# Gate and up of a block-quantized feed-forward as three products of 12-bit parts

## The chip, the cores and the metric

The program runs on one core of a Trainium2 chip. The core has five engines that run at the same time, each through its own queue in order: TensorE (PE) for matrix products, VectorE (DVE), ScalarE (ACT) and GpSimd (POOL) for elementwise work, and SyncE (SP), which here issues the DMA transfers. They wait for each other through semaphores. The metric is the time of one execution in microseconds (us) on the device. The kernel before takes 665.8 us, the median of three runs (665.08 to 667.82).

## The reference

`x` is 4 x 2048 tokens of 256 features. What is computed, cut to what matters:

```
xn   = layernorm(x)
s    = linear attention of xn over the tokens of a batch     (L2-normed Q, K; V; gamma)
gate = q(xn) @ q(w_gate).T          # 256 -> 704
up   = q(xn) @ q(w_up).T            # 256 -> 704
h    = silu(gate) * up
g    = silu(q(h) @ q(w_down).T)     # 704 -> 256
out  = x + (xn + gamma * weighted) * g
```

`q` is a blockwise 4-bit quantization and back: each block of 16 values is divided by its largest magnitude / 6, rounded to the grid 0, 0.5, 1, 1.5, 2, 3, 4, 6 and multiplied by the scale again. The result of `q` is a float32 number: a grid value times a float32 scale. `h` is quantized from the results of gate and up, so a gate or up that is off by a rounding can move a value of `h` to another grid point.

## The kernel before

The 8192 tokens are cut into 32 groups of 256 tokens (two tiles `t` of 128; NG = 8 groups a batch). A main loop `for s in range(3, N - 1)` runs a software pipeline by hand: the schedule is exactly the order of the program, and each engine works its own instructions in that order. In iteration `s` the parts of different groups are worked on:

- gate and up of group s+1 in six pieces (`pieces`, `gate_up`, L436): 2 token tiles x 3 chunks of columns (512, 512 and 384, gate and up interleaved by 64). A piece is 2 float32 products over the 256 features (the profile shows each float32 product as two instructions) into one of two PSUM banks of `ps_gu`. ACT then takes silu of the gate half (`si`, L451) and copies the up half (`up`, L453), POOL multiplies them into `h` (L455).
- the scaling of h of group s-1 (`scale_h`, L371): on DVE the largest magnitudes per block (`largest`, L151) of h and of the tokens of group s+3, the reciprocal, and h times it (`over`, L177, tile `y_h`); the same for the tokens (`y_x`).
- the rounding to the grid: ACT makes a 16-bit short of y (`short`, L210, tiles `t_h` and `t_x`), DVE four 16-bit operations (`on_grid`, L222 to L226), once for h and once for the tokens.
- the turn from tokens on the partitions to features on the partitions: the 16-bit grid values go through a DMA transpose each (`turn_q`, L415, tiles `qt_h`, `qt_x`); the scales are transposed on PE (`turn_scales`), written to DRAM (`there`) and read back spread over 16 rows of each block (`se`, L402).
- DVE multiplies the turned grid values by the spread scales: `rescale_x` (L419, tile `xqt`, group s+2) and `rescale_h` (L429, tile `hqt`, group s-2).
- down of group s-3 (`down`, L465): 12 float32 products of 256 columns (24 instructions), then silu on ACT (`gate_of`, L481).
- attention: `gram_step` (L327) for group s+3, `turn_xn` (L344) transposes its tokens; every eighth iteration the generator `attention` starts, which makes the batch's matrix M, advanced one step at each `turn()`; `preset` (L504) and `attend` (L511) for group s-7, then the product with the gate on DVE (`gated`, L521), the sum with x on POOL (`finish`, L528) and the store. `statistics`, `deviations` and `normalize` make the layer norm of later groups (mostly DVE, POOL and ACT).

Groups 0 to 4 are prepared ahead of the loop beside the weights: their tokens are quantized directly and turned on PE (`turn_xq`). The weights of gate and up are quantized in three chunks (`scale_gu`, `rounded`) and turned on PE into the tile `wgu` (`turn_gu`). After the loop a written-out end finishes the last groups.

All DMA transfers but one are issued by SP in program order: loads of x, the second load of x for the last sum (`xl`), the scales to DRAM and back, the transposes, the stores.

Of the kernel before, what the change touches and what calls it, by code (L numbers as in the profile page):

```python
# [10 lines left out]
F16 = mybir.dt.float16  # L11
AF = mybir.ActivationFunctionType
ALU = mybir.AluOpType
# [6 lines left out]
F16_EXPONENT = 0x7C00  # L20
DOWN = 1.0 - 3 * 2.0**-24
# [3 lines left out]
def kernel(  # L25
# [14 lines left out]
):  # L40

# [31 lines left out]
    ps_gu = ctx.enter_context(tc.tile_pool(name="ps_gu", bufs=2, space=bass.MemoryType.PSUM))  # L73
    ps_od = ctx.enter_context(tc.tile_pool(name="ps_od", bufs=2, space=bass.MemoryType.PSUM))
# [11 lines left out]
    def load_x(n: int):  # L86
        if n < N:
            xt = tok.tile([P, T, L], F32, tag="x", name=f"x_{n}", bufs=6)
            nc.sync.dma_start(xt, group_of(x, n))
            x_sb[n] = xt  # L90
# [3 lines left out]
    def reload_x(n: int):  # L94
        if 0 <= n < N:
            x_last[n] = tok.tile([P, T, L], F32, tag="xl", name=f"xl_{n}", bufs=3)
            nc.sync.dma_start(x_last[n], group_of(x, n))
# [5 lines left out]
    for j0, nb in chunks:  # L103
        w = tok.tile([P, HF], F32, tag="h", name=f"wgu_n{j0}", bufs=4)
# [25 lines left out]
    wd_n = tok.tile([P, NS * P], F32, tag="se", name="wd_n", bufs=2)[:, 0:HF]  # L130
# [12 lines left out]
    for i in range(5):  # L143
        xn = const.tile([P, T, L + 1], F32, tag=f"xn{i}", name=f"xn{i}")
        nc.gpsimd.memset(xn[:, :, L : L + 1], 1.0)
        xns.append(xn)
# [20 lines left out]
    def over(src: bass.AP, inv: bass.AP, F: int, kind: str, nm: str, sc=None):  # L167
# [5 lines left out]
        a = src.shape[1]  # L173
        most = T * L if kind == "x" else HF
        tag, bufs = {"x": ("yx", 2), "h": ("yh", 1), "w": ("hqt", 2)}[kind]
        y = tok.tile([P, most], F32, tag=tag, name=f"y_{nm}", bufs=bufs)[:, 0:F]
# [4 lines left out]
            inv.rearrange("p (a n) -> p a n", a=a).unsqueeze(3).to_broadcast([P, a, F // a // BLK, BLK]),  # L181
# [3 lines left out]
        return sc, y, F, kind, nm  # L185

    def scaled(src: bass.AP, F: int, kind: str, nm: str, multiplier=nc.vector):
        n, a = F // BLK, src.shape[1]
        most = T * L if kind == "x" else HF
        sc = small.tile([P, most // BLK], F32, tag="scx" if kind == "x" else "sch", name=f"sc_{nm}")[:, 0:n]  # L190
        largest(sc, src)
        inv = inverse(sc, nm)
        if multiplier is nc.vector:
            return over(src, inv, F, kind, nm, sc)
        nc.vector.tensor_scalar(inv, inv, DOWN, None, ALU.mult)
        y = tok.tile([P, most], F32, tag="hqt", name=f"y_{nm}", bufs=2)[:, 0:F]
        multiplier.tensor_tensor(
            y.rearrange("p (a n k) -> p a n k", a=a, k=BLK),
            src.rearrange("p a (n k) -> p a n k", k=BLK),
            inv.rearrange("p (a n) -> p a n", a=a).unsqueeze(3).to_broadcast([P, a, n // a, BLK]),  # L200
            ALU.mult,
        )
        return sc, y, F, kind, nm

    def short(state):
        sc, y, F, kind, nm = state
        most = T * L if kind == "x" else HF
        t = tok.tile([P, most], F16, tag="tx" if kind == "x" else "th", name=f"t_{nm}", bufs=2)[:, 0:F]
        upper = y.bitcast(BF16).rearrange("p (f two) -> p f two", two=2)[:, :, 1]
        nc.scalar.activation(t, upper, AF.Copy, scale=1.0 + 2.0**-9)  # L210
        return t

    def on_grid(state, t):
# [5 lines left out]
        sc, y, F, kind, nm = state  # L219
        most = T * L if kind == "x" else HF  # L220
        m = tok.tile([P, most], BF16, tag="mx" if kind == "x" else "mh", name=f"m_{nm}")[:, 0:F]
# [7 lines left out]
    def rounded(state, t, multiplier=nc.vector) -> bass.AP:  # L229

        return rescaled(state, on_grid(state, t), multiplier)

    def rescaled(state, q, multiplier=nc.vector) -> bass.AP:
        sc, y, F, kind, nm = state
        multiplier.tensor_tensor(
            y.rearrange("p (n k) -> p n k", k=BLK),
            q.rearrange("p (n k) -> p n k", k=BLK),
            sc.unsqueeze(2).to_broadcast([P, F // BLK, BLK]),
# [3 lines left out]

    def inv_sqrt(dst: bass.AP, v: bass.AP, nm: str):

        first = inv_sqrt_first(v, nm)
        inv_sqrt_steps(dst, v, *first)
# [89 lines left out]
    def turn_xn(n: int):  # L336
# [8 lines left out]
        xt = tok.tile([P, KC, GT], F32, tag="xnt", name=f"xnt_{n}", bufs=11)  # L345
# [6 lines left out]
    def scale_x(n: int):  # L352
        return scaled(tokens(n), T * L, "x", f"x{n}")

    def xqt_tile(n: int):
        tag, bufs = ("gate", 7) if n < 4 else ("xqt", 2)
        xqt[n] = tok.tile([P, T, KC, P], F32, tag=tag, name=f"xqt_{n}", bufs=bufs)
        return xqt[n].rearrange("p t c k -> p (t c k)")

    def turn_xq(n: int, xq: bass.AP):  # L360
# [4 lines left out]
        evict(xqt_tile(n), tp)  # L365
# [3 lines left out]
    scales, spread_sc, turned = {}, {}, {}  # L369

    def scale_h(n: int, m: int = N):  # L371
# [12 lines left out]
        inv_x[n] = inv[:, NIC * CB :]  # L384
        return over(src, inv[:, 0 : NIC * CB], HF, "h", f"h{n}")

    inv_x = {}

    def scale_x_of(n: int, h: int):
        return over(tokens(n), inv_x.pop(h), T * L, "x", f"x{n}")  # L390

    def turn_scales(key):
# [8 lines left out]
        se = tok.tile([P, NS * P], F32, tag="se", name=f"se_{key}", bufs=2)[:, 0 : n * BLK]  # L401
# [7 lines left out]
        se = se.rearrange("p (g t) -> p g t", t=P)  # L409
# [650 lines left out]
```

## Time and profile before

| | |
|---|---|
| median of the runs | 665.8 us |
| the profiled execution | 666.58 us |
| its span, first to last instruction | 664.8 us |
| granted TensorE clock | 0.997 |
| busy: PE, DVE, POOL, ACT | 639.3, 528.7, 320.5, 286.6 us |
| gate/up products (L442), 768 instructions | 315.9 us |
| down products (L469), 768 instructions | 171.0 us |
| start of loop iterations 3, 7, 29 (by the chain) | 85.35, 162.75, 586.58 us |

All times are of one profiled execution. A group in the profile reads: line, engine, operation, what it writes <- what it reads, shapes, count | busy time in total, mean ns of one | idle time of the engine just before it and what ended most of it. Matrix products are pipelined, so their mean ns overlap; the distance between starts tells what one costs in a stream. The chain follows back from the last instruction to what released each step.

### The profile page before, as it was taken

What the parts mean: (1) busy time and instruction counts of PE and PEld (TensorE: products, weight loads), DVE (VectorE), ACT (ScalarE), POOL (GpSimd) and SP (SyncE); (2) the same over time, 40 slices, a digit from 0 to 9 for tenths busy, and PEclk for the clock granted to TensorE, in tenths of its full rate; (3) what the DMA queues carried; (4) which work ended last, traced back from release to release, by engine and by line L of the source; (5) the groups of instructions that cost most, each with busy time, mean ns of one, the idle gap of its engine ahead of it and who ended that gap; (6) DMA issues with size and microseconds to landing.
All of it is one profiled execution on the core that took longest, in us unless ns stands there. A gap on an engine that the chain in (4) does not pass through costs nothing.

```text
span 664.8 us, 8117 instructions
## 1 busy us (share of the span) xinstructions
PE 639.3 (96%) x2486; PEld 435.3 (65%) x2486; DVE 528.7 (80%) x911; ACT 286.6 (43%) x701; POOL 320.5 (48%) x545
## 2 busy tenths in 40 slices
PE   3799999999999999999999999999999999999997
PEld 2446556656766666767666666766676666666886
DVE  6998997879866887867969786885997777888752
ACT  2366654344444444344453444444344444433230
POOL 5567445271635526264463636256263736537122
PEclk9999999999999999999999999999999999999999
DMA  9200488857489777764877888749778757884882
GB/s 228 77 17 0 54 101 138 117 53 85 103 122 140 140 115 108 127 99 119 137 112 101 135 125 130 120 121 141 84 113 126 111 113 114 120 125 72 150 176 97
DMA packets 86232, 74.19 MB, mean 112 GB/s; under 512 B 64076, under 2 KB 70444, under 8 KB 86188
## 3 DMA queue, kind: packets, MB, share of 16 engines
q1 hardware_dynamic: 85916, 73.40, 68.3%
q8 instruction: 20, 0.33, 0.2%
q10 hardware_dynamic: 272, 0.26, 0.1%
q14 instruction: 24, 0.20, 0.1%
HBM read 48.30 MB, written 10.27 MB: 88 GB/s over the span
## 4 chain that ended last, share of the span: by engine, by line
PE 83%; DVE 6%; POOL 3%; DMA 3%; ACT 2%; issue 1%; SPq 0%; DVEq 0%; ACTq 0%; POOLq 0%
PE gu L442 40%; PE dn L469 23%; PE at L511 8%; PE gram L327 5%; PE px L575 2%; PE tp_xn L344 2%; PE pm L661 1%; DMA qt_x<-t_x 1%; DMA wv_sb<-in_L_attn_Wv_dram 1%; DMA wgu_n<-in_L_ffn_w_gate_dram 1%; PE pa L640 1%; DMA x<-in_L_attn_x_dram 1%; POOL isq_r_ln L262 1%; PE tp_sc L396 0%; POOL h L455 0%
## 5 line engine op out<-in xcount | busy, mean ns | idle before, releaser
L442 PE MATMUL gu<-wgu,xqt 128*128 128x512 f32 (+1 forms) x768 | 315.9, 560 | 2.2 <-ACT xqt L314 2.2
L455 POOL TENSOR_TENSOR h<-si,up 128x256 f32<-128x256 f32 (+1 forms) x192 | 163.2, 857 | 274.4 <-ACT up L453 274.1
L442 PEld LDWEIGHTS gu<-wgu,xqt 128*128 128x128 f32 x768 | 143.0, 191 | 135.4 <-issue 105.4
L469 PE MATMUL dn<-wdt,hqt 128*128 128x256 f32 x768 | 171.0, 379 | 0.0
L469 PEld LDWEIGHTS dn<-wdt,hqt 128*128 128x128 f32 x768 | 144.2, 190 | 18.9
L451 ACT ACTIVATE si<-gu 128x256 f32<-128x256 f32 (+1 forms) x192 | 70.2, 366 | 192.2 <-PE gu L442 187.4
L419 DVE TENSOR_TENSOR xqt<-qt_x,se 128x512 f32<-128x512 bf16 x27 | 26.0, 961 | 72.0 <-DMA qt_x<-t_x 67.3
L453 ACT COPY up<-gu 128x256 f32<-128x256 f32 (+1 forms) x192 | 67.7, 353 | 0.0
L327 PEld LDWEIGHTS gram<-xn 128*128 128x128 f32 x256 | 44.0, 194 | 27.6 <-ACT xn L305 11.4
L511 PE MATMUL at<-M,xnt 128*128 128x256 f32 x256 | 59.7, 379 | 0.0
L429 DVE TENSOR_TENSOR hqt<-qt_h,se 128x1408 f32<-128x1408 bf16 x32 | 53.8, 1680 | 7.0 <-DMA qt_h<-t_h 7.0
L327 PE MATMUL gram<-xn 128*128 128x257 f32 (+1 forms) x256 | 48.9, 335 | 9.2 <-ACT xn L305 9.2
L177 DVE SCALAR_TENSOR_TENSOR y_h<-h,inv_h 128x1408 f32<-128x1408 f32 x32 | 54.7, 1711 | 2.5 <-ACT t_h L210 1.4
L210 ACT ACTIVATE t_h<-y_h 128x1408 f16<-128x1408 bf16 x32 | 44.3, 1385 | 17.5 <-DVE y_h L177 17.5
L151 DVE TENSOR_REDUCE scs<-h 128x88 f32<-128x1408 f32 x32 | 51.6, 1612 | 0.0
L511 PEld LDWEIGHTS at<-M,xnt 128*128 128x128 f32 x256 | 46.7, 190 | 6.7
L314 ACT COPY sct<-tp_sc 120x128 f32<-120x128 f32 (+1 forms) x32 | 8.4, 265 | 92.7 <-PE tp_sc L396 92.7
L305 ACT ACTIVATE xn<-x,shift,rstd 128x256 f32<-128x256 f32 x64 | 35.0, 597 | 28.2 <-POOL shift L295 28.2
L528 POOL TENSOR_TENSOR gate<-gate,xl 128x512 f32<-128x512 f32 x26 | 35.6, 1370 | 22.4 <-DVE gate L521 22.4
L225 DVE TENSOR_TENSOR t_h<-m_h,t_h 128x1408 bf16<-128x1408 bf16 x32 | 31.1, 972 | 1.1
L226 DVE TENSOR_TENSOR t_h<-t_h,m_h 128x1408 bf16<-128x1408 bf16 x32 | 28.5, 892 | 1.1
L164 DVE RECIPROCAL inv_h<-scs 128x120 f32<-128x120 f32 (+1 forms) x32 | 27.9, 873 | 1.1
(145 smaller groups left out, 662.9 us busy)
## 6 DMA issues: line engine op xcount, KB each, us to landing
se<-there SPq DMA_DIRECT2D x27, 960.0 KB
x<-in_L_attn_x_dram SPq DMA_DIRECT2D x32, 256.0 KB
out_dram<-gate SPq DMA_DIRECT2D x31, 256.0 KB
xl<-in_L_attn_x_dram SPq DMA_DIRECT2D x26, 256.0 KB
se<-there SPq DMA_DIRECT2D x5, 704.0 KB
there<-sct SPq DMA_DIRECT2D x27, 60.0 KB
wd_n<-in_L_ffn_w_down_dram SPq DMA_DIRECT2D x1, 704.0 KB
wgu_n<-in_L_ffn_w_up_dram SPq DMA_DIRECT2D x2, 256.0 KB
```

The source lines that it names most:

```text
L151: nc.vector.tensor_reduce(sc, src.rearrange("p a (n k) -> p a n k", k=BLK), AX.X, ALU.max, apply_absolute_value=True)
L177: nc.vector.scalar_tensor_tensor(y.rearrange("p (a n k) -> p a n k", a=a, k=BLK), src.rearrange("p a (n k) -> p a n k", k=BLK), DOWN, inv. ...
L210: nc.scalar.activation(t, upper, AF.Copy, scale=1.0 + 2.0**-9)
L327: nc.tensor.matmul(grams[b][:, o : o + L + 1 - c * P], xn[:, t, c * P : (c + 1) * P], xn[:, t, c * P : L + 1], start=(g == 0 and t == 0 an ...
L429: nc.vector.tensor_tensor(ht, turned.pop(("h", n)).rearrange("p g t -> p (g t)"), spread_sc[n][:, 0:NIC, :].rearrange("p g t -> p (g t)"), ...
L442: nc.tensor.matmul(gu[:, : nb * P], xqt[n][:, t, c, :], wgu[:, c, j0 * P : (j0 + nb) * P], start=(c == 0), stop=(c == KC - 1),)
L451: nc.scalar.activation(si[:, :nb, :], pair[:, :, 0, :], AF.Silu)
L453: nc.scalar.copy(up[:, :nb, :], pair[:, :, 1, :])
L455: nc.gpsimd.tensor_tensor(hs[n][:, o : o + nb * 64], si[:, :nb, :].rearrange("p j f -> p (j f)"), up[:, :nb, :].rearrange("p j f -> p (j f)"),
L469: nc.tensor.matmul(od[:, t, :], hqt[n][:, t * half + i, :], wdt[:, t * (half + 1) + i, :], start=(i == 0), stop=(i == half),)
L511: nc.tensor.matmul(ready[n][:, t, :], xt[:, c, t * P : (t + 1) * P], M[:, c, :], start=False, stop=(c == KC - 1), skip_group_check=True,)
L528: adder.tensor_tensor(gate, gate, x_last.pop(n), ALU.add)
```

## The change

**Gate and up.** For most groups (`SPLIT = 5, 5, 6`: from group 5 on for the first two chunks of columns, from group 6 on for the third) each float32 product is replaced by three products of type float32r. The tokens' tile f is split into a = f times (1 - 2^-13) rounded to float32r (`part_a`, ACT), b = f - a (`part_b`, POOL) and m = a - 2^12 b (`part_m`, DVE). The weights are split once, chunk by chunk, into three tiles `wgu[0..2]` (`split_gu`, six passes of ACT and four of POOL per chunk). A piece is now begun (`gu_begin`: a and b against the first two weight parts, four instructions), rescaled in PSUM by ACT (times 1 + 2^-12), and ended later in the program (`gu_end`: two more products of m, then si, up and h as before). Earlier groups keep the float32 products against untouched tiles `wp`.

**Shared operations.** h of group s-1 and the tokens of group s+3 lie side by side in one tile `y` of 1920 columns, so `on_grid` and the DMA transpose run once over both. The short is made in three parts. `rescale_x` moves from DVE to POOL and writes f. `spread_scales` is separated from `turn_scales` and stands behind the transpose and behind `rescale_h` of the group before it.

**Order and memory.** The loop's order is new: pieces are begun one ahead of the one that is ended, down is cut into four quarters between them, attend into two. Attention's generator has 13 steps in place of more, with five `turn()` in each iteration. PSUM: three banks for gate/up, one for down. Several tiles have fewer buffers (x 5, xn 4, h 3, hqt 1, se 1, gate 6, xl 2, xnt 10, M and mrow 1).

```diff
+SHORT = 1.0 - 2.0**-13
+STEP = 2.0**12
...
     def rescale_x(n: int, key: int):
-        nc.vector.tensor_tensor(
-            xqt_tile(n),
...
+        f = tok.tile([P, T * L], F32, tag="f", name=f"f_{n}", bufs=2)
+        nc.gpsimd.tensor_tensor(f, turned[key][:, HF:], spread_sc[key][:, HF:], ALU.mult)
+        return f
...
+    def part_a(n: int, f: bass.AP):
+        a = part(n, 0)
+        nc.scalar.activation(a, f, AF.Copy, scale=SHORT)
+        xqt[n] = [a]
+
+    def part_b(n: int, f: bass.AP):
+        b = part(n, 1)
+        nc.gpsimd.tensor_tensor(b, f, xqt[n][0].bitcast(F32), ALU.subtract)
+        xqt[n].append(b)
+
+    def part_m(n: int, f: bass.AP):
+        a, b = xqt[n]
+        m = part(n, 2)
+        nc.vector.scalar_tensor_tensor(m, b.bitcast(F32), -STEP, a.bitcast(F32), ALU.mult, ALU.add)
...
+    def gu_begin(n: int, t: int, i: int):
...
+            pairs = [(xqt[n][k][:, t, c, :], wgu[k][:, c, cols]) for k in range(2) for c in range(KC)]
+        for k, (x_k, w_k) in enumerate(pairs):
             nc.tensor.matmul(
...
+                gu[:, : nb * P], x_k, w_k, start=(k == 0), stop=(k == len(pairs) - 1), skip_group_check=True
             )
+        if split:
+            nc.scalar.activation(gu[:, : nb * P], gu[:, : nb * P], AF.Copy, scale=1.0 + 1.0 / STEP)
+        return n, t, i, gu
+
+    def gu_end(state):
...
+            for c in range(KC):
+                nc.tensor.matmul(
+                    gu[:, : nb * P],
+                    xqt[n][2][:, t, c, :],
+                    wgu[2][:, c, cols],
+                    start=False,
...
+        for c in range(KC):
+            nc.scalar.activation(c_[c], wp[i, c][:, 0 : nb * P], AF.Copy, scale=SHORT)
+            nc.gpsimd.tensor_tensor(rest[c], wp[i, c][:, 0 : nb * P], c_[c].bitcast(F32), ALU.subtract)
...
+        u0 = gu_begin(*pairs[0])
+        if f >= 0:
+            preset(f)
         gram_step(s + 3)
...
+        y_h = scale_h(s - 1, s + 3)
+        th = grid_tile(y_h, f"h{s - 1}")
+        u1 = gu_begin(*pairs[1])
+        gu_end(u0)
+        down(s - 3, 0)
+        u2 = gu_begin(*pairs[2])
+        gu_end(u1)
+        down(s - 3, 1)
+        short_part(th, y_h, 0, FF)
+        u3 = gu_begin(*pairs[3])
+        short_part(th, y_h, FF, HF)
+        if more_x:
+            short_part(th, y_h, HF, NS * P)
         turn()
...
+        gu_end(u2)
+        if parts_x:
+            xs = rescale_x(s + 2, s - 2)
+        down(s - 3, 2)
+        u4 = gu_begin(*pairs[4])
+        gu_end(u3)
+        down(s - 3, 3)
+        turn_scales(s - 1)
+        u5 = gu_begin(*pairs[5])
+        if parts_x:
+            part_a(s + 2, xs)
+            part_b(s + 2, xs)
+        gate_of(s - 3)
+        next(parts, None)
+        gu_end(u4)
+        if f >= 0:
+            attend(f, 0)
...
+        turn_q(s - 1, on_grid(th, f"h{s - 1}"))
...
+        normalize(s + 4)
+        if f >= 0:
+            attend(f, 1)
+        gu_end(u5)
         turn()
+        rescale_h(s - 2)
+        spread_scales(s - 1)
+        if parts_x:
+            part_m(s + 2, xs)
+        if f >= 0:
+            close(f)
+        turn_xn(s + 3)
+        store()
+        turn()
```

## The prediction

> **What bounds the kernel now.** I read the page's busy times, its chain of work that ended last, and its costliest groups first.
>
> ```profile
> PE 639.3 (96%) x2486; PEld 435.3 (65%) x2486; DVE 528.7 (80%) x911; ACT 286.6 (43%) x701; POOL 320.5 (48%) x545
> ...
> PE 83%; DVE 6%; POOL 3%; DMA 3%; ACT 2%; issue 1%; SPq 0%; DVEq 0%; ACTq 0%; POOLq 0%
> ...
> L442 PE MATMUL gu<-wgu,xqt 128*128 128x512 f32 (+1 forms) x768 | 315.9, 560 | 2.2 <-ACT xqt L314 2.2
> ```
>
> PE is the bound and gate/up is half of it. Then the chain in order of time, one loop iteration:
>
> ```profile
> 218.06 3.43 PE gu L442 x8
> 221.50 1.31 PE gram L327 x8
> 222.81 6.01 PE gu L442 x16
> ...
> 229.26 5.18 PE dn L469 x24
> ...
> 234.55 1.73 PE at L511 x8
> 236.28 3.43 PE gu L442 x8
> ```
>
> A plain iteration is 18.22 us and PE has no gap. Two windows (columns: length, busy PE, PEld, DVE, ACT, POOL, clock, DMA share, GB/s) give the other engines:
>
> ```profile
> 199.84:354.63 154.79, 154.54 (x601) 105.97 (x600) 124.68 (x215) 67.26 (x169) 73.88 (x125) 1.00 0.74 121
> ...
> 199.84:218.06 18.22, 18.22 (x71) 12.30 (x70) 12.98 (x23) 8.10 (x21) 10.52 (x21) 1.00 0.90 129
> 218.06:236.28 18.22, 18.22 (x71) 12.30 (x70) 16.27 (x22) 8.07 (x21) 6.74 (x7) 1.00 0.73 128
> ```
>
> A batch (8 groups) is 154.79 us: 8 x 18.22 plus 9.0 of attention on PE. DVE is busy 14.6 us in a plain iteration (mean of the two rows), plus 124.7 - 8 x 14.6 = 7.7 a batch for attention. Last, the timelines of POOL and DVE:
>
> ```profile
> 220.60 0.76 POOL L455 TENSOR_TENSOR h<-si,up 128x256 f32<-128x256 f32 x1 [2.95 <-ACT up L453]
> 220.69 2.15 DVE L429 TENSOR_TENSOR hqt<-qt_h,se 128x1408 f32<-128x1408 bf16 x1
> ...
> 372.50 1.32 POOL L528 TENSOR_TENSOR gate<-gate,xl 128x512 f32<-128x512 f32 x1
> ...
> 372.72 1.24 DVE L223 TENSOR_SCALAR m_x<-m_x 128x512 bf16<-128x512 f16 x1
> ```
>
> The hqt product takes 1.62 at its median and m_x 0.29. Each started while a POOL operation ran and was 0.53 and 0.95 longer: these DVE operations wait for POOL.
>
> **PE's part.** A gate/up product of 512 columns is two instructions of 3.43/8 = 0.429 us. No float32r is in the trace. The nearest one-pass row is the bf16 512-column product that opens banks: two of them take 0.59 us, one 0.38, so 0.21 apart, half of a float32 instruction. The Trainium skill ("FP8 and Floating Point Precision", TensorE Precision Notes) says that true FP32 is four passes and that a reduced reading truncates to FP22; 2 x 0.429 is four times 0.21, which agrees, and one pass for the reduced reading is taken from there (no run shows it). Its price is between 0.21 and 0.429; I take 0.215, and 0.162 for 384 columns. A weight load with each product hides: gram's products are 1.31/8 = 0.164 apart with a load each (at worst its 0.19 would set the pace of 12 of them: +0.3 an iteration). A group then needs 24 x 0.215 + 12 x 0.162 = 7.1 for 9.44, so a plain iteration 15.9 on PE. The saving is 27 x 2 x (3.43 - 2.58) + 26 x (2.58 - 1.94) = 62 us of PE.
>
> **What is added elsewhere, per iteration.** ACT: four rescalings of 512 columns in PSUM (0.60 each, like gate<-dn) and two of 384 (0.49), part_a 0.60, a third start of the shorts 0.2: 4.2, so 8.1 becomes 12.3, below 15.9. POOL: rescale_x and part_b, 1.27 each by the gate addition's row: 8.6 becomes 11.2. DVE: rescale_x leaves (0.61 start to start), part_m comes (0.61, like y_x). The grid operations at 1408 and 512 are 2.85 + 1.43 start to start; at 1920, by their slope, 3.66: 0.6 saved, 14.0 left. SP issues one transpose where it issued two (4.7 and 4.8 us of SP each), the spread of scales behind it and not ahead: its landing is due only at the next iteration's rescale_x, and I charge nothing; with that cover gone, part_a holds ACT's queue. Attention's yields and PSUM buffers: the same work in 13 steps, five an iteration; nothing.
>
> **Waits that are new.** On PE the last two products of a piece wait for ACT's rescaling in PSUM, and every later product is queued behind them. Between a piece's first products and its last stand the next piece's first four (0.86) and a quarter of down (5.18/4 = 1.30): 2.2 us, against 0.3 of hand-over (gu's end to si, 219.62 to 219.88) and 0.6 of ACT, so nothing, while ACT comes within 1.3 us; after that each microsecond is PE's. On ACT, whose queue is in order, the first half short waits for DVE's y_h, with piece 3's rescaling behind it; and part_a waits for POOL's rescale_x, with gate_of, si and up of pieces 4 and 5, normalize, xnt and the next group's first rescaling behind it, 4.4 us by their rows. preset waits for the gated of the group before. On SP the store of `there` and the spread stand in the same queue as the loads of x and xl and the output; the spread of scales has one buffer now and waits for rescale_h. The three gate/up banks are free in time: a bank's si and up are read two pieces before its next use.
>
> **The cycle that PE no longer hides.** In the new order ACT makes the shorts of h and of the tokens before gate and up of piece 2. So on_grid starts when the last short ends, and POOL's h of piece 2, rescale_x, h of piece 3 and part_b all come behind that, while DVE runs on_grid and rescale_h without a break. From one on_grid to the next: on_grid 3.66, rescale_h 1.53, part_m 0.61 (it needs part_b), gated 0.59, largest to reciprocal 3.43, y_h 1.55, then ACT 3.0 (two half shorts 0.80, a rescaling 0.60 between, the token short 0.64, hand-overs); statistics hide beside ACT. Sum 14.4, below PE's 15.9 while DVE never waits. Here a rule speaks against the change: the Trainium skill ("SBUF — State Buffer", SBUF: two separate sides) calls the port pair of DVE and GpSimd an exclusive lock, held for the whole instruction. By the rule, four waits cost 2 x 0.73 + 2 x 1.27 = 4.0 and the cycle is 18.4, which by the sum below would end at 672. By the rows a delayed DVE operation loses 0.5 to an h and 0.95 to a 512-wide one, since its start-up overlaps: 2.9, and the cycle is **17.3**. The lower end is no wait that matters, 15.9. I take 17.3: the rows are of this program.
>
> PE feels it through part_b. The next group's first product with b waits for it, and piece 3's (counted from 0), after which ACT rescales it and makes the last shorts, comes to its end 0.43 + gram 1.31 + pieces and quarters of down 6.2 = 8.0 later, then 2.4 of ACT to the next on_grid: 10.4 plus the end of part_b. If part_b gets the port before rescale_h it ends 6.8 after on_grid's start (17.2, the same); behind rescale_h 8.3 (18.7).
>
> **The sum**, from the span of 664.8:
> - Up to 85.35: splitting the first weights adds 3.6 on ACT and four POOL operations (5.1); DVE is busy 74.4 of these 85, so half of POOL's counts: +2.5.
> - Iterations 3 to 6 (85.35 to 162.75 by the chain): no gated, 4 x 16.7, two more splits 4, attention 7.7: 78.5 for 77.4, +1.
> - Iterations 7 to 28 (to 586.58): 22 x 17.3 + 2.3 x 7.7 = 398.3 for 423.8: -25.5.
> - From 586.58: two iterations of 14.6 (no gram), pa, pm and pq 4, then the last h: four DVE phases ahead of it 14, its own scaling, short and grid 8, scales through DRAM 12, rescale 1.6, down 5.2, end 3: 77 for 78.2, -1.
>
> Span 641.8. The profiled execution took 666.6 and the runs' median is 665.8, 1.0 above the span: **643**.
>
> **Rivals.** (1) **PE stays the bound**: the queues settle so that POOL falls beside tensor_reduce, statistics and gated. For it: in the kernel before DVE loses only about 0.8 an iteration (group means less medians) though POOL works 8.6. Against: on_grid and rescale_h are 5.2 unbroken and four POOL operations are bound to follow the same short. 22 x 15.9 + 2.3 x 9.0 is 370.5, -53; iterations 3 to 6 69, -8.5; the end -1: **603**. (2) **part_b goes behind rescale_h** and PE waits for it every iteration: 22 x 18.7 + 17.7 = 429, +5.3; iterations 3 to 6 +6.7; start and end +1.5: **679**, slower. It decides from 18.2 an iteration, when part_b ends 7.8 after on_grid's start. For it: part_a stands behind piece 5's rescaling on ACT, so part_b reaches POOL 5.8 after on_grid began, just as rescale_h starts. (3) **float32r is not one pass**: at 0.429 a group needs 14.2, +4.8 an iteration over before, 27 of them: **794**; it loses from 0.29 an instruction. (4) The loads' order undoes it: the spread lands late, rescale_x and ACT behind it; about 665.
>
> **How the numbers follow.** Forecast (own range 622 to 660) 0.52; rival 1 0.24; rival 2 0.15; rival 3 0.03; rival 4 0.06. 0.5% is 3.3 us, about what a measurement here tells from no change. Faster: 0.50 of the forecast, 0.24, 0.03 of rival 2 and 0.02 of rival 4, 0.79; within 0.5%: 0.02, 0.02 of rival 2 and 0.03 of rival 4, 0.07; slower: the rest, 0.14. Eight in ten: from inside rival 1 (606: about 0.09 lies below, waits make it more than 603) to the lower part of rival 2 (672: 0.11 lies above).
>
> **What would show it.** Gate/up instructions from group 5 on 0.21 apart; PE busy near 577; plain iterations of about 17.3 with PE waiting for part_b or for ACT's rescaling; grid operations, hqt and part_m lengthened beside POOL; the spread landed before rescale_x. Iterations of 15.9 make rival 1 right; PE waiting 1.5 us or more per iteration for POOL, rival 2.

## The result and the profile after

The changed kernel takes 706.4 us (705.41 to 709.21) where the kernel before takes 665.9 (665.08 to 667.82) beside it: a ratio of 1.061 (95% interval 1.057 to 1.065), 6% slower. The forecast was 643, with eight chances in ten for 606 to 672. The profiled execution took 709.21 us, its span is 707.4.

The page of the changed kernel, busy times, chain by engine and four of the costliest groups:

```profile
PE 626.0 (88%) x2805; PEld 505.3 (71%) x2807; DVE 568.7 (80%) x804; ACT 390.5 (55%) x934; POOL 458.2 (65%) x610
...
PE 29%; POOL 22%; DMA 22%; DVE 10%; issue 10%; ACT 5%; SPq 0%; POOLq 0%; ACTq 0%; DVEq 0%
...
L471 PE MATMUL gu<-wgu,xq 128*128 128x512 f32 (+1 forms) x640 | 196.5, 425 | 35.4 <-POOL xq L439 30.5
...
L485 PE MATMUL gu<-wgu,xq 128*128 128x512 f32 (+1 forms) x320 | 99.8, 393 | 2.5 <-ACT gu L475 2.5
...
L453 DVE TENSOR_TENSOR hqt<-qt,se 128x1408 f32<-128x1408 bf16 (+2 forms) x33 | 70.6, 2141 | 8.2 <-DMA qt<-t_h 6.5
...
L439 POOL TENSOR_TENSOR xq<-f,xq 128x512 fp32r<-128x512 f32 x27 | 58.5, 2168 | 0.0
```

PE fell from 96% to 88% of a longer span, and from 83% to 29% of the chain: it is no longer the bound, and nothing else alone is. L471 is the first part of a piece (`gu_begin`): PE stood idle 30.5 us ahead of it for `part_b` (POOL, L439). L485 is the second part (`gu_end`); ACT's rescaling ahead of it cost PE 2.5 us in the whole run. `part_b` takes 2.17 us on average where the gate addition, the row from which it was priced, took 1.27 before; hqt takes 2.14 for 1.68.

The windows of two plain iterations and of a batch (same columns as before: length, busy PE, PEld, DVE, ACT, POOL, clock, DMA share, GB/s):

```profile
395.42:414.43 19.01, 16.44 (x72) 14.11 (x72) 15.62 (x24) 10.96 (x26) 11.34 (x11) 0.91 0.56 123
414.43:433.40 18.97, 18.70 (x93) 15.72 (x91) 16.80 (x15) 12.38 (x32) 17.02 (x25) 1.00 0.54 123
398.70:558.70 160.00, 147.53 (x696) 125.47 (x695) 133.93 (x183) 96.07 (x232) 113.07 (x142) 0.97 0.53 115
```

The first two windows are cut about at the starts of `part_b`. By PE's first product with part b, at 398.11, 416.68 and 435.94, two plain iterations take 37.83, so one is 18.9 for 18.22; a batch is 160.0 for 154.8. DVE's own load is under it (15.6 and 16.8), so the iteration is set by waits. The chain in order of time across one iteration, and then the timelines of POOL, DVE, SP and PE at the same place, show which:

```profile
380.34 11.86 DMA se<-there
...
393.81 1.64 POOL h L499
395.45 2.62 POOL xq L439
398.06 0.04 issue
398.11 0.73 PE gu L471 x2
```

```profile
392.34 1.50 POOL L426 TENSOR_TENSOR f<-qt,se 128x512 f32<-128x512 bf16 x1 [1.23 <-DMA se<-there]
393.81 1.64 POOL L499 TENSOR_TENSOR h<-si,up 128x256 f32<-128x256 f32 x1
395.42 2.64 POOL L439 TENSOR_TENSOR xq<-f,xq 128x512 fp32r<-128x512 f32 x1
...
389.42 1.11 DVE L229 TENSOR_SCALAR m_h<-t_h 128x1920 uint16<-128x1920 uint16 x1 [1.97 <-ACT t_h L219]
...
394.78 2.15 DVE L453 TENSOR_TENSOR hqt<-qt,se 128x1408 f32<-128x1408 bf16 x1
398.09 1.07 DVE L445 SCALAR_TENSOR_TENSOR xq<-xq,xq 128x512 fp32r<-128x512 f32 x1 [1.15 <-POOL xq L439]
...
380.34 0.61 SPq L407 DMA_DIRECT2D se<-there  x1
...
394.82 0.72 PE L471 MATMUL gu<-wgu,xq 128*128 128x512 f32 x2
398.11 0.73 PE L471 MATMUL gu<-wgu,xq 128*128 128x512 f32 x2 [2.57 <-POOL xq L439]
398.67 2.67 PE L327 MATMUL gram<-xn 128*128 128x257 f32 x8
```

Read from the top: POOL's `rescale_x` (tile f) waits 1.23 us for the spread of scales, which SP issued at 380.34 behind the `rescale_h` of the iteration before. `part_b` comes to POOL at 395.42, 0.64 us after DVE has started `rescale_h` (hqt); it holds its place for 2.64 us, where it needs 1.26 at its fastest, and ends at 398.06, 8.6 us after `on_grid` started (389.42). PE has run the two products with part a and stands still for 2.57 us. The eight gram products after that take 2.67 us; after a wait of 0.24 (below) they take 1.47.

The next iteration is different. The same places in the timelines of POOL, DVE and PE:

```profile
414.43 2.19 POOL L439 TENSOR_TENSOR xq<-f,xq 128x512 fp32r<-128x512 f32 x1
...
410.01 0.66 DVE L229 TENSOR_SCALAR m_h<-t_h 128x1920 uint16<-128x1920 uint16 x1 [1.92 <-ACT t_h L219]
...
415.41 2.70 DVE L453 TENSOR_TENSOR hqt<-qt,se 128x1408 f32<-128x1408 bf16 x1
...
416.68 0.73 PE L471 MATMUL gu<-wgu,xq 128*128 128x512 f32 x2 [0.24 <-POOL xq L439]
```

Here the scales are there in time, `part_b` comes 4.42 us after `on_grid` and 0.98 ahead of `rescale_h`, and PE waits 0.24. Plain iterations of the two kinds come in turn: from one `on_grid` to the next it is 20.59 us (389.42 to 410.01) and 17.24 (410.01 to 427.25). Of the 22 iterations from 7 to 28, `part_b` starts behind `rescale_h` in 13.

Where the time went, by the first gram product of groups 6, 10 and 31 (each a little into loop iterations 3, 7 and 28), for both kernels and all the runs below, in us:

| run | before group 6 | 6 to 10 | 10 to 31 | 31 to the end | span | median |
|---|---|---|---|---|---|---|
| before | 88.6 | 77.4 | 401.4 | 97.4 | 664.8 | 665.9 |
| after | 89.2 | 94.8 | 412.5 | 110.9 | 707.4 | 706.4 |
| e1 products alone | 89.0 | 76.8 | 389.1 | 96.5 | 651.3 | 650.1 |
| e2 order alone | 87.3 | 83.4 | 404.1 | 102.3 | 677.1 | 681.2 |
| e3 part_m first | 89.4 | 90.7 | 408.8 | 108.6 | 697.5 | 700.3 |
| e4 gram first | 89.2 | 92.8 | 400.2 | 106.6 | 688.9 | 692.1 |
| e5 no part_b | 90.5 | 88.4 | 377.6 | 105.9 | 662.3 | 662.2 |
| e6 spread x early | 88.9 | 93.0 | 396.5 | 109.5 | 687.8 | 691.3 |
| e7 store behind | 88.9 | 92.2 | 411.4 | 102.2 | 694.8 | 697.1 |
| e8 parts early | 89.1 | 91.8 | 397.4 | 103.5 | 681.8 | 680.9 |
| e9 deviations late | 89.0 | 98.4 | 412.6 | 105.9 | 705.9 | 706.8 |
| e10 with start and tail | 89.8 | 95.7 | 414.4 | 96.3 | 696.2 | 697.6 |
| e11 part_b on DVE | 89.5 | 91.7 | 393.7 | 101.0 | 675.9 | 678.0 |
| e12 roots first | 89.4 | 88.4 | 384.7 | 96.5 | 659.0 | 661.4 |

The loss of 42.6 in the span is 17.4 in the first four iterations, 11.2 in the loop and 13.5 in the end. The forecast had +1, about -24 and about -2 there. (In e4 gram comes earlier in the iteration, so its marks do too.)

### The profile page after: what moved, and what is told of

It reads as the page before. It is cut to its first block, busy times and chain, and to the rows that moved or that the text cites. A ratio compares the mean times of both kernels' runs of the same rounds, so it can differ in the third digit from the quotient of the medians.

```text
span 707.4 us, 9043 instructions
## 1 busy us (share of the span) xinstructions
PE 626.0 (88%) x2805; PEld 505.3 (71%) x2807; DVE 568.7 (80%) x804; ACT 390.5 (55%) x934; POOL 458.2 (65%) x610
## 4 chain that ended last, share of the span: by engine, by line
PE 29%; POOL 22%; DMA 22%; DVE 10%; issue 10%; ACT 5%; SPq 0%; POOLq 0%; ACTq 0%; DVEq 0%
DMA se<-there 18%; PE gu L471 11%; POOL h L499 10%; PE dn L519 7%; POOL xq L439 6%; PE gram L327 4%; PE gu L485 2%; POOL f L426 1%; PE px L619 1%; PE pa L681 1%; DMA xl<-in_L_attn_x_dram 1%; DMA qt<-t_h 1%; DVE hqt L453 1%; POOL isq_r_n L260 1%; ACT gu L475 1%
## 5 line engine op out<-in xcount | busy, mean ns | idle before, releaser
L499 POOL TENSOR_TENSOR h<-si,up 128x256 f32<-128x256 f32 (+1 forms) x192 | 195.2, 1026 | 150.7 <-ACT up L497 150.7
L471 PE MATMUL gu<-wgu,xq 128*128 128x512 f32 (+1 forms) x640 | 196.5, 425 | 35.4 <-POOL xq L439 30.5
L475 ACT ACTIVATE gu<-gu 128x512 f32<-128x512 f32 (+1 forms) x160 | 87.6, 547 | 136.4 <-PE gu L471 134.1
L471 PEld LDWEIGHTS gu<-wgu,xq 128*128 128x128 f32 x640 | 116.0, 195 | 60.9 <-POOL xq L439 39.2
L485 PE MATMUL gu<-wgu,xq 128*128 128x512 f32 (+1 forms) x320 | 99.8, 393 | 2.5 <-ACT gu L475 2.5
L495 ACT ACTIVATE si<-gu 128x256 f32<-128x256 f32 (+1 forms) x192 | 69.8, 364 | 21.7 <-PE gu L471 17.8
L219 ACT ACTIVATE t_h<-y_h 128x704 f16<-128x704 bf16 (+2 forms) x86 | 63.6, 770 | 31.5 <-DVE y_h L184 31.4
L453 DVE TENSOR_TENSOR hqt<-qt,se 128x1408 f32<-128x1408 bf16 (+2 forms) x33 | 70.6, 2141 | 8.2 <-DMA qt<-t_h 6.5
L229 DVE TENSOR_SCALAR m_h<-t_h 128x1920 uint16<-128x1920 uint16 (+1 forms) x32 | 23.1, 722 | 63.3 <-ACT t_h L219 63.3
L485 PEld LDWEIGHTS gu<-wgu,xq 128*128 128x128 f32 x320 | 59.6, 191 | 12.4 <-ACT gu L475 3.9
L327 PEld LDWEIGHTS gram<-xn 128*128 128x128 f32 x256 | 51.2, 224 | 20.6 <-ACT xn L305 11.2
L439 POOL TENSOR_TENSOR xq<-f,xq 128x512 fp32r<-128x512 f32 x27 | 58.5, 2168 | 0.0
L471 PE MATMUL gu<-wp,xqt 128*128 128x512 f32 (+1 forms) x120 | 53.1, 588 | 2.2 <-ACT xqt L314 2.2
L426 POOL TENSOR_TENSOR f<-qt,se 128x512 f32<-128x512 bf16 x27 | 44.4, 1643 | 13.4 <-DMA se<-there 13.4
```

The lines of the kernel that those rows point to most:

```text
L219: nc.scalar.activation(t[:, lo:hi], upper[:, lo:hi], AF.Copy, scale=1.0 + 2.0**-9)
L327: nc.tensor.matmul(grams[b][:, o : o + L + 1 - c * P], xn[:, t, c * P : (c + 1) * P], xn[:, t, c * P : L + 1], start=(g == 0 and t == 0 an ...
L439: nc.gpsimd.tensor_tensor(b, f, xqt[n][0].bitcast(F32), ALU.subtract)
L453: nc.vector.tensor_tensor(ht[:, lo:hi], turned[n][:, lo:hi], spread_sc[n][:, lo:hi], ALU.mult)
L471: nc.tensor.matmul(gu[:, : nb * P], x_k, w_k, start=(k == 0), stop=(k == len(pairs) - 1), skip_group_check=True)
L475: nc.scalar.activation(gu[:, : nb * P], gu[:, : nb * P], AF.Copy, scale=1.0 + 1.0 / STEP)
```

## The experiments

All but the first edit are made on the changed kernel; e8 to e12 contain earlier ones, as said at each. In the edits `...` stands for lines that are not shown.

**e1, the products without the new order.** The kernel before, with six one-pass instructions for each piece.

```diff
-        for c in range(KC):
+        for k in range(3 * KC):
+            c = k % KC
             nc.tensor.matmul(
...
-                start=(c == 0),
-                stop=(c == KC - 1),
+                start=(k == 0),
+                stop=(k == 3 * KC - 1),
```

(`wgu` and `xqt` are tiles of type float32r.)

> The kernel before, in its old order, with each gate/up product made of six one-pass float32r instructions instead of two float32 ones (the parts are not formed: the same rounded operands are multiplied three times over, so what is left out is the splitting into parts and the rescaling, and the values are not those of the reference). Theory (the instructions are cheap, the new order loses the gain): a 512-column instruction near 0.22, a plain iteration 15.9 to 16.5, the whole 600 to 625 us. Rival (DVE and POOL hold any order at about 18 us an iteration): 645 to 665 us.

650.1 us, ratio 0.975 (0.972 to 0.979): the rival, in the lower part of its range. In a stream the starts of the 512-column products lie 0.23 apart, so the instructions are cheap (all 32 groups have them here). But the old order turns 40 us less of busy PE (598.9 for 639.3) into 16: plain iterations range from 16.5 to about 19. Two of its waits (us in total, times, longest) say what takes over:

```profile
DVE xqt L420 <- DMA qt_x<-t_x: 53.7, 18, 6.4
...
PE gram L328 <- ACT xn L306: 18.8, 8, 7.6
```

DVE waits for the second transpose of each iteration, and PE for a normalize that waits for POOL. So in the old order, too, something other than PE held many iterations above 16.5.

**e2, the new order without the products.** Float32 products; no parts of tokens or weights, no rescaling.

```diff
-    SPLIT = 5, 5, 6
+    SPLIT = 99, 99, 99
...
-            part_a(s + 2, xs)
-            part_b(s + 2, xs)
+            xqt[s + 2] = None, None, None, xs.rearrange("p (t c k) -> p t c k", t=T, c=KC)
```

> The changed kernel with float32 products: its order, its shared grid operations and its single transpose stay; the parts of the tokens and of the weights, part_b, part_m and the rescalings go. Theory (part_b behind rescale_h is what holds the loop, order and sharing cost only at start and end): PE again full in the loop at 18.2 to 18.5 an iteration, start of the loop and tail some 15 us worse than before, the whole 675 to 690 us. Rival (the order itself, its single-buffered spread of scales and its store queue, holds the loop): 695 to 715 us, with PE waiting in the loop. If neither start nor tail lose: 666 us.

681.2 us, ratio 1.021 (1.018 to 1.023), as the theory said. In the loop PE is full at 18.2 an iteration: 2.7 us lost over 21 iterations. The order costs 6.0 in the first four iterations and 4.9 in the end.

**e3, part_m ahead of rescale_h on DVE.**

```diff
+        if parts_x:
+            part_m(s + 2, xs)
         rescale_h(s - 2)
         spread_scales(s - 1)
-        if parts_x:
-            part_m(s + 2, xs)
```

> The changed kernel with part_m ahead of rescale_h on DVE, so that DVE waits for part_b and cannot hold its port with rescale_h. Theory (part_b waits for rescale_h): part_b takes 1.3 to 1.6 instead of 2.2 us at its median, PE's wait for it falls from 39 + 30 us to under 20, an iteration loses 1 to 1.5 us: 675 to 690 us. Rival (the spread of scales, which waits for rescale_h, sets the cycle): rescale_h and the spread come 1.5 to 2 us later and so does rescale_x: 705 to 740 us.

700.3 us, ratio 1.052 (1.048 to 1.056): between the two expectations. The row of part_b (least, median and largest time in ns) and two waits of this run:

```profile
L439 POOL TENSOR_TENSOR xq<-f,xq x27: 1261/1278/2179, 110.3 to 626.9; 128x512 fp32r<-128x512 f32 x27
...
POOL f L426 <- DMA se<-there: 38.1, 23, 3.5
...
PE gu L471 <- POOL xq L439: 12.2, 18, 1.4
```

With no hqt to stand behind, part_b takes 1.28 at its median (2.20 in the changed kernel), and PE's wait for it falls from 30.5 to 12.2. This shows that DVE's operation beside it, and nothing in part_b itself, makes it long. What is won is mostly given back: rescale_h comes later, the spread of scales waits for it, rescale_x now waits 38.1 us for scales (13.4 in the changed kernel), and part_m, now ahead of rescale_h on DVE, waits 61.2 us for part_b (23.8).

**e4, gram ahead of the next group's first products on PE.**

```diff
+        gram_step(s + 3)
         u0 = gu_begin(*pairs[0])
         if f >= 0:
             preset(f)
-        gram_step(s + 3)
```

> The changed kernel with gram's eight products (1.31 us) ahead of the next group's first gate/up products on PE, so that they fill the wait for part_b. Theory (PE waits for part_b and all that follows on PE is late by that wait): an iteration loses about 1.3 us, 26 of them: 670 to 680 us. Rival (the cycle is closed by the transfer of scales and by DVE, PE's wait is only its slack): 700 to 708 us.

692.1 us, ratio 1.038 (1.034 to 1.042): 14 us better, half of what the theory asked for. An iteration fell by 0.6 instead of 1.3, because gram needs tokens that are normalized late; the wait for part_b itself is almost gone (us in total, times, longest):

```profile
PE gram L327 <- ACT xn L305: 34.9, 16, 7.8
...
PE gu L471 <- POOL xq L439: 1.9, 1, 1.9
```

**e5, no part_b.** Part a stands in for part b.

```diff
-        b = part(n, 1)
-        nc.gpsimd.tensor_tensor(b, f, xqt[n][0].bitcast(F32), ALU.subtract)
-        xqt[n].append(b)
+        xqt[n].append(xqt[n][0])
```

> The changed kernel without part_b: part a of the tokens is used in its place (left out is the subtraction on POOL; the values are then not those of the reference). Theory (PE waits in every iteration for part_b, which stands behind rescale_h on the shared port): PE then waits for part_a at most, POOL loses 2.2 us an iteration, iterations of 16.3 to 17.3, the whole 655 to 675 us. Rival (the spread of scales or ACT's rescalings hold the loop whatever POOL does): iterations stay above 18.3 and the whole above 690 us.

662.2 us, ratio 0.992 (0.989 to 0.995). 27 POOL operations of 1.26 us, 34 us of an engine that was busy 65%, make 44 us of the whole. Three things go with them: PE's wait for part_b, part_m's wait for it, and what it took from DVE's operations beside it. Two iterations of this run:

```profile
505.00:521.40 16.40, 16.27 (x81) 13.93 (x79) 14.23 (x14) 11.16 (x29) 14.13 (x23) 1.00 0.56 127
521.40:537.80 16.40, 16.40 (x81) 14.04 (x81) 16.09 (x21) 11.37 (x29) 10.71 (x9) 1.00 0.55 127
```

PE is full again, with an iteration of 16.7 (next group's first products at 505.32, 522.15 and 538.81). hqt is still long (2.06 on average): the lengthening of DVE's operations by itself is hidden, as long as nothing that PE waits for stands behind it.

**e6, the tokens' scales spread at once.** The spread is split; 256 KB for the tokens go out ahead of the transpose, into two buffers of their own (three small tiles give up one buffer each).

```diff
         turn_scales(s - 1)
+        if more_x:
+            spread_x(s - 1)
```

> The changed kernel with the spread of scales split in two: the tokens' scales (256 KB) are spread at once into a buffer of their own, two of them, ahead of the transpose in SP's queue; only h's scales (704 KB) still wait for rescale_h. Theory (part_b behind rescale_h on the port holds the loop and the spread only arrives within that slack): POOL's wait for scales ahead of rescale_x, 13.4 us in all, goes, the iteration stays between 18.3 and 19.0: 697 to 707 us. Rival (the single-buffered spread sets the cycle, which is what the chain's 18% would mean): 1 us or more an iteration, 670 to 690 us.

691.3 us, ratio 1.036 (1.030 to 1.040), 15 below the changed kernel and between the two expectations. The spread was not only slack: 0.8 us an iteration came from it. With it early part_b starts ahead of rescale_h in every plain iteration of the loop. PE still waits for it (17.8 us), and plain iterations are 17.0 and 19.1 in turn. In the longer ones it is DVE that is full (18.75 of 19.06 busy, the third figure):

```profile
382.15:401.21 19.06, 17.99 (x89) 15.36 (x88) 18.75 (x24) 12.77 (x33) 14.44 (x11) 1.00 0.57 137
```

The last of the statistics there ends at 401.30, the last short at 399.94, and on_grid, which needs that short and a free DVE, starts at 401.21.

**e7, one store of the end behind the last scales.**

```diff
     close(f)
     close(f + 1)
-    store()
     down(n - 2, 0)
...
     turn_q(n, on_grid(th, f"h{n}"))
+    store()
```

> The changed kernel with one store in the tail moved behind the last group's scales, their spread and their transpose in the order of SP's queue. Theory (SP waits for POOL's gate addition, which waits for a reload of x, while the last scales are ready at about 672): the scales of group 31 leave 8 to 9 us earlier and all after them: 697 to 700 us. Rival (the last h's chain is bound by its down products and gates, or the transposes then land no earlier): 703 to 707 us.

697.1 us, ratio 1.043 (1.040 to 1.046), as the theory said. SP's queue in the end of the changed kernel, and then of this run:

```profile
667.19 1.74 SPq L106 DMA_DIRECT2D xl<-in_L_attn_x_dram  x3
680.54 0.82 SPq L582 DMA_DIRECT2D out_dram<-gate  x2
681.41 0.49 SPq L400 DMA_DIRECT2D there<-sct  x1
684.02 0.61 SPq L407 DMA_DIRECT2D se<-there  x1
684.75 2.20 SPq L420 DMA_TRANSPOSE qt<-t_h  x1
```

```profile
661.77 2.12 SPq L106 DMA_DIRECT2D xl<-in_L_attn_x_dram  x3
666.84 0.32 SPq L400 DMA_DIRECT2D there<-sct  x1
671.39 0.61 SPq L407 DMA_DIRECT2D se<-there  x1
672.06 2.33 SPq L420 DMA_TRANSPOSE qt<-t_h  x1
```

In the changed kernel SP stands from 669 to 680.54 at a store, whose gate addition waits for a reload of x (POOL waits 13.9 us for it), and the last group's scales and transpose stand behind that store. With the store moved, the last part falls from 110.9 to 102.2; in e10, e11 and e12, which have this too, it is 96.3, 101.0 and 96.5, for 97.4 in the kernel before.

**e8, the parts made early.** On top of e6, rescale_x is POOL's first work of an iteration, part_a stands ahead of the shorts, part_b and part_m are on DVE in the gap where it waits for them.

```diff
+        if parts_x and s > 3:
+            xs = rescale_x(s + 2, s - 2)
         if s % 2:
             deviations(moments)
...
-        nc.gpsimd.tensor_tensor(b, f, xqt[n][0].bitcast(F32), ALU.subtract)
+        nc.vector.tensor_tensor(b, f, xqt[n][0].bitcast(F32), ALU.subtract)
...
         down(s - 3, 1)
+        if parts_x and s > 3:
+            part_a(s + 2, xs)
+            part_b(s + 2, xs)
+            part_m(s + 2, xs)
         short_part(th, y_h, 0, FF)
```

> The split spread of the run with the tokens' scales first, and the parts of the tokens made earlier, for group s+2 already before the shorts: rescale_x is POOL's first work of an iteration, part_a stands ahead of the short on ACT, part_b and part_m are on DVE in the gap in which it waits for the shorts (2.2 us an iteration). Nothing of the computation is left out. Theory (part_b's place on the port is what cost the gain; ACT's rescalings, the spread and the rest of the new order are cheap): PE never waits for a part, the iteration falls to 16.5 to 17.3, the whole to 650 to 675 us, under the kernel before. Rival (what holds the loop is DVE with POOL on one port, and the parts only change places): iterations of 18 to 18.5, 690 to 700 us.

680.9 us, ratio 1.017 (1.013 to 1.022). PE waits for a part once (5.1 us, in iteration 4), but the loop's iterations are now 16.4 or 20 to 22. POOL and ACT in a long one:

```profile
411.76 1.59 POOL L293 TENSOR_SCALAR shift<-mv 128x4 f32<-128x4 f32 x1
422.08 2.78 POOL L509 TENSOR_TENSOR h<-si,up 128x256 f32<-128x256 f32 x4
...
422.84 0.38 ACT L505 ACTIVATE si<-gu 128x256 f32<-128x256 f32 x1 [5.79 <-POOL h L509]
```

Between the two POOL rows lie the small operations of the layer norm's square roots, 10.3 us; four h stand behind them, and ACT waits 5.79 us for a free `si`.

**e9, the square roots behind the h of piece 2.**

```diff
-        if s % 2:
-            deviations(moments)
         turn()
         u0 = gu_begin(*pairs[0])
...
+        if s % 2:
+            deviations(moments)
         down(s - 3, 2)
```

> The run with the parts made early, with the square roots of the statistics (20 small operations on POOL, 10.3 us from 411.8 to 422.1 in that run's odd iteration, ahead of all of its h products) put behind the h of piece 2. Nothing is left out. Theory (odd iterations of 20 to 22 us are ACT waiting for a si buffer that POOL's h frees, even ones of 16.4 show what the loop can do): odd iterations fall to 16.5 to 18, the whole 645 to 663 us, faster than the kernel before. Rival (odd iterations are long for another reason, such as the transpose that lands late): 672 to 685 us.

706.8 us, ratio 1.058 (1.054 to 1.062): a miss, 26 worse than e8. ACT's wait for `si` went, but normalize then waits for the roots, and gram for normalize:

```profile
ACT xn L305 <- POOL shift L295: 66.0, 15, 6.9
...
PE gram L327 <- ACT xn L305: 44.8, 16, 7.6
```

**e10, e9 with changes to start and end.** e7's store; rescale_h of group 0 ahead of the statistics of groups 7 and 8; part_m straight behind part_b in iteration 3.

```diff
     turn_q(1, on_grid(th, "h1"))
-    moments = statistics(7, 8)
     rescale_h(0)
...
         y_h = scale_h(s - 1, s + 3)
+        if s == 3:
+            moments = statistics(7, 8)
```

> The run with the square roots behind piece 2, with the tail's store behind the last scales as in the run that moved it, and at the start rescale_h of group 0 ahead of the statistics of groups 7 and 8, which go behind y_h, and part_m straight behind part_b in iteration 3. Nothing is left out. Theory (start and tail lose by the order alone, apart from part_b): 8 us from the tail and 4 to 8 us from iterations 3 and 4, so 12 to 16 us below the run without them. Rival (they are paced by the splitting of the weights on ACT and POOL and by the chain of the last h): less than 6 us.

697.6 us, ratio 1.045 (1.040 to 1.049), 9 below e9, between the two expectations: 9.6 from the end, 2.7 from iterations 3 to 6, 1.8 given back in the loop. The end gained about what e7 gained (8.7); the start hardly moved.

**e11, part_b on DVE straight behind on_grid,** with e6's spread, e7's store and, at the start, rescale_h of group 0 first.

```diff
-        nc.gpsimd.tensor_tensor(b, f, xqt[n][0].bitcast(F32), ALU.subtract)
+        nc.vector.tensor_tensor(b, f, xqt[n][0].bitcast(F32), ALU.subtract)
...
         turn_q(s - 1, on_grid(th, f"h{s - 1}"))
+        if parts_x:
+            part_b(s + 2, xs)
```

> The changed kernel with part_b on DVE, straight behind on_grid and ahead of rescale_h, and part_m as before; with the tokens' scales spread early, the tail's store behind the last scales, and at the start rescale_h of group 0 ahead of the statistics of groups 7 and 8. rescale_x, part_a and the square roots keep their places. Nothing is left out. Theory (only part_b's place on the port cost the loop its gain; without it iterations took 16.4 to 17.2): DVE pays 0.7 more, iterations of 17.0 to 17.8, 8 us less tail, 2 us less start: 650 to 668 us. Rival (any part made between on_grid and the next group's products holds PE, on whichever engine): above 675 us.

678.0 us, ratio 1.018 (1.015 to 1.021): the rival. In the loop this is 2.8 us better than e6, which has part_b on POOL, so the engine matters little as long as part_b stays in this stretch. PE still waits for part_b (19.2 us ahead of its weight loads), and DVE, which runs on_grid, part_b, hqt and part_m in one row, is 40% of the chain.

**e12, e8 with the square roots ahead of rescale_x,** where the changed kernel has them, and with the start and end of e10.

```diff
-        if s % 2:
+        if s % 2 and s > 3:
             deviations(moments)
+        if parts_x and s > 3:
+            xs = rescale_x(s + 2, s - 2)
```

> The run with parts made early and the same tail and start, but with the square roots of the statistics on POOL ahead of rescale_x, where they stand in the changed kernel, so that they fall beside DVE's reductions. Nothing is left out. Theory (the odd iterations of 20 us came from the 10.3 us of small POOL operations between rescale_x and the h products, the 19 us ones of the later place from normalize waiting for them): odd iterations 17 to 18.5, even ones 16.4, 655 to 670 us. Rival (odd iterations stay at 19 or more wherever the roots stand): above 678 us.

661.4 us, ratio 0.9924 (0.990 to 0.9947): 0.8% below the kernel before, a small gain but outside its interval, with nothing of the computation left out. Of the odd iterations some fell to 17 and 18, others stayed at 19 to 20.6, so the expectation on them held in part.

```profile
PE 47%; DVE 28%; POOL 11%; issue 7%; ACT 5%; DMA 2%; SPq 0%; ACTq 0%; DVEq 0%; POOLq 0%
```

## Why the prediction was wrong

**The step that failed is the end of part_b, and with it the spread of scales, put at nothing.** The prediction had PE's cycle as 10.4 plus the end of part_b after on_grid's start, with two values for that end: 6.8 with the port before rescale_h, 8.3 behind it. It took 6.8 for every iteration, although it said that part_b reaches POOL 5.8 after on_grid began, just as rescale_h starts. The trace has the early end in every second plain iteration: part_b ends 6.6 after on_grid, the next on_grid is 10.6 later, and the cycle of 17.24, in which ACT's first short waits 1.14 for DVE's y_h, is the forecast's 17.3. In the other kind part_b comes 6.0 after on_grid, 0.64 behind rescale_h's start at 5.36, and ends at 8.6; the next on_grid is then 12.0 later and not 10.4, since PE runs slowly after its wait (last section). That makes 20.6. The two kinds have a mean of 18.9, near the 18.7 of rival 2 (given 0.15) and above its point of decision of 18.2. But rival 2 had 18.7 in every iteration, so that its value came out so close is in part luck.

**What puts part_b behind rescale_h is the spread of scales, "I charge nothing".** Its issue waits for rescale_h, it takes 11.9 us (380.34 to 392.20), and after a short iteration rescale_x stands 1.23 behind it. Without that wait part_b would have come at about 394.2, ahead of rescale_h at 394.78 (an estimate from these starts). After a long iteration the scales are there in time, and the next one is short. e6 is the test: with the spread early part_b is ahead of rescale_h in the plain iterations, and the loop gains 16.0 (412.5 to 396.5). Rival 4 was thus part of the outcome, not an alternative to the rest; e3 shows the two coupled.

**The rest of the loop.** Without part_b (e5) 21 iterations take 377.6, 23.8 less than before, where the forecast had about 24 with it. So of the 34.9 that e5 gains, the early spread alone gains 16.0, and plain iterations of e6 are still 18.0 in the mean for 17.3. There the prediction's "statistics hide beside ACT" does not hold: in every second iteration DVE is full for 19.06. e3, e4 and e11 lie in between. part_b lies on a closed path (PE's pieces, ACT's shorts, on_grid, part_b, PE), and taking it out of that stretch, with the spread early, helped more (e12: 384.7) than giving it another engine in the same stretch (e11: 393.7).

**The rule and the row.** The Trainium skill ("SBUF — State Buffer", SBUF: two separate sides) has the pair held for the whole instruction; the prediction set this at 4.0 us of waits an iteration and took 2.9 from the rows. From on_grid's start to part_m's end it is 3.66 + 1.53 + 0.61 = 5.8 unhindered. In the short iteration it takes 9.09 (410.01 to 419.10), 3.3 more. In the long one it takes 9.74, 3.9 more, of which 1.15 is part_m's wait for part_b by semaphore and 2.8 is left. For DVE the rows' 2.9 was thus near the truth, and the short cycle, which DVE sets, came out as forecast. What the rows, read for DVE's loss only, left out is POOL's side. part_b, recorded from 395.42, ends 1.13 us after hqt's end at 396.93: it stood for all of hqt and then took its own time, as the rule has it, and PE waited for it.

**Iterations 3 to 6, +1 forecast, +17.4 measured.** The order is 6.0 of it (e2), part_b 6.4 (after less e5), and the 5.0 between e2 and e5 is what else the parts add there, the splitting of the weights among it; that split was not run alone. The order's share begins in iteration 3, in the changed kernel's timeline of PE:

```profile
96.31 2.93 PE L519 MATMUL dn<-wdt,hqt 128*128 128x256 f32 x6 [3.85 <-DVE hqt L453]
```

The first quarter of down now stands ahead of the pieces that used to cover the wait for the first hqt, and every later product of PE stands behind it. e2, with the order alone, waits there too (2.76). The prediction counted work in these iterations, and no wait.

**The end, -1 forecast, 13.5 longer.** It added phases of DVE, and did not name what stands ahead of the last scales in SP's queue. e7 puts 8.7 on one store; the other 4.8 were not run apart (they are gone in e10 and e12, not in e11).

**PE's part.** One pass was right: the instruction costs 0.232 in the stream (0.93 for four, forecast 0.215), about a quarter of a float32 product (0.86), so rival 3 is out. It costs 0.175 at 384 columns (forecast 0.162): 24 x 0.232 + 12 x 0.175 = 7.7 for a group instead of 7.1, most of the difference between 15.9 and the 16.7 of e5. PE's busy time is 626, not 577, since it also runs slowly after waits (below); in e1 it is 598.9. The rescaling on ACT hides, as predicted. Rival 1 asked for 603, and no run came near: e5, with PE full in the loop, still has the dearer instruction, 11 us more than before in iterations 3 to 6 and 8.5 more in the end.

## What to carry to other kernels

An operation that moves to an engine with time to spare is not priced by its load: ask between which two events it stands, and whether its result closes a path back to those events. Where two orders of two events lie within a few tenths of a microsecond and decide a bound, the chances belong near half and half; here both orders came in turn, in cycles of 17.2 and 20.6 us. A transfer that one iteration issues and the next one needs can be in time after a long iteration and late after a short one, so a single iteration of the trace does not show the loop. In a queue that issues transfers in order, each store that waits for an engine delays every load and transpose written behind it, so a new order is checked at the start and at the end as closely as in the loop.

## What the runs showed of the hardware that was not expected

PE's granted clock drops after waits that are short, and the prediction had no term for this. In the changed kernel's loop, gram's eight products, which come right behind the wait for part_b, took 2.3 to 2.8 us after each of five waits of 2.56 or 2.57 us, 1.5 to 2.8 after six waits of about 1.9 (five in the loop from iteration 7 on, one in iteration 5), and 1.47 after the one of 1.61. The window behind the wait at 398.11, and the two microseconds that follow it:

```profile
398.10:402.10 4.00, 3.99 (x13) 3.37 (x14) 3.96 (x5) 1.17 (x2) 2.77 (x3) 0.58 0.62 143
402.10:404.10 2.00, 2.00 (x11) 1.70 (x10) 1.93 (x3) 1.14 (x3) 0.08 (x1) 0.98 1.00 234
```

The granted clock is 0.58 in the mean of the four microseconds, and 0.50 from 398.77 to 402.19. From gram's start to the first `gu_end` it takes 3.88 us (398.67 to 402.55) against 2.23 in the iteration before (379.42 to 381.65), so this wait of 2.57 cost 1.65 more than itself, and the loss is handed on to the shorts and to on_grid. The Trainium skill ("TensorE: Matmul & The Clock Gate", Part 1) gives an idle window of about 3.4 us for the drop; here 2.56 was enough each time, and 1.9 some of the time. What goes with the drop in this trace is how busy PE was in the 3.41 us before it, not the length of one wait. Each single stretch of low clock is 3.41 us long, and all their starts lie on one grid of that step. From 100 to 660 us PE was busy for 25 to 45% of each full-clock step that preceded a low one (0.84 us from 395.36 to 398.77), and for 52% or more of every other full-clock step. This is read from one trace: e7's has one step each way that breaks it (43% with no drop, 59% with one).
